# Five `h` tiles instead of four, the `y` sums in the spent half of `u`, a shorter gate, and 360 fill products instead of 480

## The chip, the cores and the metric

The kernel runs on one core of a Trainium2 chip. The metric is the device time of one execution in microseconds. Before the change it is 3912.99 us, the median of three runs (3912.96 to 3919.06). A core has five engines with instruction streams of their own, each worked off in order: PE (TensorE: matrix products; its weight loads are listed as PEld), DVE (VectorE), ACT (ScalarE), POOL (GpSimd) and SP (SyncE), which in this kernel issues every DMA. Engines wait for each other through semaphores.

## What is computed

The input `x` is eight sequences of 512 tokens with 256 channels, all in float32. Four residual layers follow each other:

```python
x = x + attn_a(layernorm(x))   # latent attention, 16 heads, rotary tables, causal softmax
x = x + ffn(layernorm(x))      # gate, up and down products (704 wide), inputs and weights rounded to FP4 blocks
x = x + attn_b(layernorm(x))   # a state-space layer, both directions in time
x = x + ffn(layernorm(x))      # the same weights again
```

The change lies in the state-space layer:

```python
xz = layernorm(x) @ in_w;  xs, z = split(xz)          # 512 channels each
for each direction d (forward, backward):
    xc = silu(causal_conv(xs))
    dt, B, C = split(xc @ xproj_w)                    # 64, 16 and 16 columns
    dt = softplus(dt @ dt_w + dt_b)
    h[t] = exp(dt[t] * A) * h[t-1] + dt[t] * B[t] * xc[t]     # 512 channels x 16 states
    y_d[t] = sum over the 16 states of h[t] * C[t]  +  xc[t] * D_skip
y = concat(y_fwd, y_back) @ merge_w * silu(z)         # silu(z) is the gate
x = x + residual + y @ out_w
```

## The kernel before

**Threads.** The program is written as Python generators that are interleaved: one for attention (`attention`, `heads`), one for feed-forward layers, the input half of the state-space layer and its merge (`ffns`, `mamba_pre`, `merge`), and one for the scans (`ssm`, with `ssm_prep` for what a scan needs). While sequence `b` is scanned, attention for `b + 3` and feed-forward layers of other sequences are spread between its steps. What they record is not yet the final order.

**The planner.** `issue_in_order` (L138) takes the whole recorded program and makes the order of each engine by hand, as a list scheduler. It derives dependences from the memory that instructions read and write, gives each a duration from a table (`cost`, L96) and a rank (the longest remaining path), and lets the instruction with the highest rank that is ready go next. It then ties each engine to that order. So any change of a duration class, of a ring's depth or of a dependence can reorder all engines.

**Rings.** Tiles come from rings, by tag: a tile waits until all users of the tile that many places before it are done. `h` has four tiles of 128x1024 float32, `u` three, `rep0` and `rep1` three each, `tmpB` three, `yt` one of 128x512. In PSUM, the eight banks are split as `pa` 2, `pb` 2, `a` 2, `y` 1, `ub` 1.

**A scan step.** For each sequence and direction there are four column blocks `m` of 128 channels, each with eight steps of two states: 512 steps in all. A step does the following:

- SP loads the rows of B and C for two states, replicated to 128 partitions (`rep0`, `rep1`; L1059, 512 KB each).
- DVE multiplies `ub` (a PSUM copy of `u = dt * xc`, made by ACT at L1077 at the start of each `m`) by `rep0` into an `h` tile (L1081).
- ACT makes two exponentials (L1084), and DVE runs two scans in place in the `h` tile (L1086 the forward direction, L1088 the backward one).
- POOL multiplies the tile by `rep1` (L1095).
- PE adds its eight 128x128 parts, transposed, into the bank `y` (L1098). The `h` tile is free then.

After eight steps ACT copies `y` into the tile `yt` (L1102), PE transposes it back in four products into a bank `a` (L344, called at L1105), DVE adds `xc * D_skip` (L1106), and SP stores the result.

**Preparation of a scan.** `ssm_prep` loads the convolved input of a direction as two `u` tiles of two column blocks each (L1015, two loads for each sequence and direction, 32 in all). The x-projection (L314 into `a`, with `tmpA` and `u`) reads both of them. Then dt follows (L1038 to L1051), and `u` is multiplied by dt in place (L1052). A `u` tile is used by two column blocks, `m % 2` of 0 and 1; its last reader is the copy into `ub` (L1077) of the second.

**The gate.** In `mamba_pre`, for the four column blocks of `z`, a product lands in a `pb` bank `o`. ACT makes `th = tanh(0.5 * (o + bias))` (L965) and `zb = o + bias` (L967), and DVE closes with `(th + 1) * zb` (L968) from two SBUF tiles. The convolution above it (`conv`, L928 to L930) already has another form: tanh, then plus one on ACT, and DVE reads PSUM.

**Fill products.** 480 products of constants (L1189, 128x512 bf16, nothing reads them) are recorded first. Their output is the first tile of the ring `y`:

```python
    FILL, FILL_FROM, FILL_GAP = 480, 70000, 600
...
    idle = psum("y")
    for _ in range(FILL):
        PE.matmul(idle.rearrange("p (a k) -> p a k", a=NT), idb, idb[:, None, :].to_broadcast([P, NT, P]), start=True, stop=True)
```

The planner gives them the lowest rank, and number `c` may not be planned ahead of 70 us + `c` * 0.6 us of its own clock.

Of the kernel before, what the change touches and what calls it, by code (L numbers as in the profile page):

```python
# [11 lines left out]
F32 = mybir.dt.float32  # L12
# [4 lines left out]
AF = mybir.ActivationFunctionType  # L17
ALU = mybir.AluOpType
AX = mybir.AxisListType

P = 128
T = 512
# [37 lines left out]


DMA_LAT = 2300


def accesses(i):
# [24 lines left out]
def ways(i):  # L90

    outer = [next((c for _, c in a.bass_ap.ap if c > 1), 1) for a in list(i.ins) + list(i.outs)]
    return max(k for k in range(1, 17) if all(x % k == 0 for x in outer))
# [44 lines left out]
def issue_in_order(tc, traced, rings, idle):  # L138
# [8 lines left out]
    hist, users, writers = {}, {}, {}  # L147
    for k, i in enumerate(ops):
        for name, lo, hi, p0, p1, _, psum, wr in acc[k]:
            h = hist.setdefault(name, [])  # L150
# [45 lines left out]
    port = [shared_port(i, a) for i, a in zip(ops, acc)]  # L196
    dma = [type(i).__name__ == "InstDMACopy" for i in ops]
    rank = [0.0] * n
    for k in reversed(range(n)):
        rank[k] = costs[k][1] * (1.2 if ops[k].engine == mybir.EngineType.DVE else 1.0) + DMA_LAT * dma[k] + max([rank[j] for j in succ[k] + behind[k]], default=0.0)  # L200
    at = [0.0] * n
    for c, k in enumerate(users[idle[0]]):
        rank[k], at[k] = -1.0, idle[1] + idle[2] * float(c)
# [9 lines left out]
    for _ in range(n):  # L213
        best = None
        for e, q in later.items():
            r, t = ready.setdefault(e, []), free.get(e, 0.0)
            while q and q[0][0] <= t:
                k = heapq.heappop(q)[1]
# [7 lines left out]
        while q and q[0][0] <= t:  # L226
            k = heapq.heappop(q)[1]
            heapq.heappush(r, (-rank[k], k))
        k = heapq.heappop(r)[1]
# [3 lines left out]
        if dma[k]:  # L233
            t = max(t, flying[0])
            m = ways(ops[k])
            lines[:m] = [max(t + 800, x) + costs[k][1] for x in lines[:m]]
            end = max(lines[:m]) + DMA_LAT - 800
            heapq.heapreplace(flying, end)
# [32 lines left out]
def tile_hybrid(ctx: ExitStack, tc: tile.TileContext, w: dict, consts: bass.AP, out: bass.AP):  # L271
    nc = tc.nc
    V, S, G, PE = nc.vector, nc.scalar, nc.gpsimd, nc.tensor
# [8 lines left out]
    cnt = [0]  # L282
    PB, TB, HB, QB, QA, HT = 2, 4, 3, 2, 2, 1
    LAG, TC, XB = 2, 3, 3
    NHB, NU, NDT, TA, RB, YT = 4, 3, 2, 2, 3, 1

    def const(shape, dt, tag):
        return cp.tile(shape, dt, tag=tag, name=tag)

    rings = {}  # L290

    def ringed(tag, bufs, t):
        rings.setdefault(tag, (bufs, []))[1].append(t.name)
        return t

    def work(shape, dt, tag, bufs=2):
        cnt[0] += 1
        return ringed(tag, bufs, wk.tile(shape, dt, tag=tag, name=f"{tag}_{cnt[0]}", bufs=bufs))
# [191 lines left out]
    def stats(src, th, twice=False):  # L490


        st = work([P, NT, 6], F32, "lnst" + th, 2)
        mv = work([P, NT, 2], F32, "lnmv" + th, 2)
        for i in range(NT):
            V.bn_stats(st[:, i, :], src[:, i, :])
        for i in range(NT):
            V.bn_aggr(mv[:, i, :], st[:, i, :])
        n = NT * (2 if twice else 1)
        ve = work([P, n], F32, "lnve" + th, 2)  # L500
        r = work([P, n], F32, "lnr" + th, 2)
        G.tensor_scalar(ve[:, :NT], mv[:, :, 1], EPS, None, ALU.add)
        if twice:
            G.tensor_scalar(ve[:, NT:], mv[:, :, 1], 1.0 + EPS, EPS * EPS, ALU.mult, ALU.add)
        newton_rsqrt(r, ve, n, th)
        return mv, r

    def shift(mv, r, th):
        nm = work([P, NT], F32, "lnnm" + th, 2)
        G.tensor_scalar(nm, mv[:, :, 0], -1.0, None, ALU.mult)  # L510
        G.tensor_tensor(nm, nm, r, ALU.mult)
        return nm

    def normalise(dst, src, r, nm):
        for i in range(NT):
            S.activation(dst[:, i, :], src[:, i, :], AF.Identity, bias=nm[:, i : i + 1], scale=r[:, i : i + 1])
# [5 lines left out]
    def token_transpose(dst, src, tag="pb"):  # L522

        for ct in range(2):
            o = psum(tag)
            for i in range(NT):
                transpose(o[:, i * P : (i + 1) * P], src[:, i, ct * P : (ct + 1) * P])
            S.copy(dst[:, ct, :], o)
# [332 lines left out]
    bin_ = const([P, 8], F32, "bin")  # L861
    binh = const([P, 8], F32, "binh")
# [69 lines left out]
    def mamba_pre(src, scr):  # L932
        xn = work([P, NT, C], F32, "fxn", 1)
        nc.sync.dma_start(xn, src.rearrange("(a p) c -> p a c", p=P))
        mv, r = stats(xn, "m", twice=True)
        nm, nm2 = shift(mv, r[:, :NT], "m"), shift(mv, r[:, NT:], "m2")
        r1 = work([P, NT], F32, "lnr1", 2)
        G.tensor_scalar(r1, r[:, :NT], 1.0, None, ALU.add)
        for i in range(NT):
            x3 = work([P, C], F32, "xrf", XB)  # L940
            S.activation(x3, xn[:, i, :], AF.Identity, bias=nm[:, i : i + 1], scale=r1[:, i : i + 1])
            nc.sync.dma_start(scr["x3"][i * P : (i + 1) * P, :], x3)
        normalise(xn, xn, r[:, NT:], nm2)
        yield
        xT = work([P, 2, T], F32, "fxT", 2)
        token_transpose(xT, xn)
        yield
        for m in range(8):
            wp = work([P, 2, P], F32, "xrf", XB)
            nc.sync.dma_start(wp, win_d[m])  # L950
            o = psum()
            for ct in range(2):
                mm(o, wp[:, ct, :], xT[:, ct, :], start=(ct == 0), stop=(ct == 1))
            if m < ND:
                xs = xsb[m % 2]
                S.activation(xs[:, 3 : 3 + T], o, AF.Identity, bias=bin_[:, m : m + 1])
                yield
                for d in range(2):
                    xb = work([P, T], F32, "tmpB", TC)
                    conv(d, m, xs, xb)  # L960
                    nc.sync.dma_start(scr["xc"][4 * d + m], xb)
                    yield
            else:
                th = work([P, T], F32, "tmpB", TC)
                S.activation(th, o, AF.Tanh, bias=binh[:, m : m + 1], scale=0.5)  # L965
                zb = work([P, T], F32, "tmpB", TC)
                S.activation(zb, o, AF.Identity, bias=bin_[:, m : m + 1])  # L967
                V.scalar_tensor_tensor(zb, th, 1.0, zb, ALU.add, ALU.mult)  # L968
                nc.sync.dma_start(scr["sz"][m - ND], zb)
                yield  # L970

# [94 lines left out]
    def ssm(b, d, scr):  # L1066


        for m in range(ND):
            if m % 2 == 0:  # L1070
                dt, u, _ = prep.pop((b, d, m // 2))
            while len(reps) < RB - 1:
                reps.append(load_rep(*todo_rep.pop(0), 0))
                repc.append(load_rep(*todo_c.pop(0), 1))
            y = psum("y")
            ub = psum("ub")
            S.copy(ub, u[:, m % 2, :])  # L1077
            for n in range(NS // 2):
                rb, rc = reps.pop(0), repc.pop(0)
                h = work([P, 2, T], F32, "h", NHB)  # L1080
                V.tensor_tensor(h, ub[:, None, :].to_broadcast([P, 2, T]), rb, ALU.mult)  # L1081
                for e in range(2):
                    a = psum("a")
                    S.activation(a, dt[:, m % 2, :], AF.Exp, scale=Aneg[:, d, m, 2 * n + e : 2 * n + e + 1])  # L1084
                    if d == 0:
                        V.tensor_tensor_scan(h[:, e], a, h[:, e], 0.0, ALU.mult, ALU.add)  # L1086
                    else:
                        V.tensor_tensor_scan(h[:, e, ::-1], a[:, ::-1], h[:, e, ::-1], 0.0, ALU.mult, ALU.add)  # L1088
                if todo_rep:
                    reps.append(load_rep(*todo_rep.pop(0), 0))  # L1090
                    repc.append(load_rep(*todo_c.pop(0), 1))
                if n == 2:
                    xp = work([P, T], F32, "xp", 1)
                    nc.sync.dma_start(xp, scr["xc"][4 * d + m])
                G.tensor_tensor(h, h, rc, ALU.mult)  # L1095
                for e in range(2):
                    for i in range(NT):
                        PE.matmul(y[:, i * P : (i + 1) * P], h[:, e, i * P : (i + 1) * P], ident,  # L1098
                                  start=(n == 0 and e == 0 and i == 0), stop=(n == NS // 2 - 1 and e == 1 and i == NT - 1), is_transpose=True)
                yield  # L1100
            yt = work([P, T], F32, "yt", YT)
            S.copy(yt, y)  # L1102
            o = psum("a")
            for q in range(NT):
                transpose(o[:, q * P : (q + 1) * P], yt[:, q * P : (q + 1) * P])  # L1105
            V.scalar_tensor_tensor(xp, xp, Dh[:, d, m : m + 1], o, ALU.mult, ALU.add)  # L1106
            nc.sync.dma_start(scr["y"][4 * d + m], xp)
# [70 lines left out]
                        pass  # L1178

    NA_, NB_, NS_ = 80, 100, 80  # L1180
    FILL, FILL_FROM, FILL_GAP = 480, 70000, 600
    PREP_AT, PREP_EV = 2, 2
    prep = {}
    af = {}
# [21 lines left out]
    first = thread_s(0)  # L1206
# [39 lines left out]
```

## Time and profile before

| what | value |
|---|---|
| median of the runs | 3912.99 us |
| profiled execution, its own time | 3908.11 us |
| its span, first to last instruction | 3906.3 us |
| mean granted PE clock | 0.903 |
| PE busy | 3215.2 us, 82% |
| DVE busy | 2953.2 us, 76% |
| POOL busy | 2111.9 us, 54% |
| ACT busy | 1740.7 us, 45% |
| DMA | 898.19 MB, mean 230 GB/s |

The profile is one execution, seen by the hardware profiler. A row of a group of instructions reads: line of the kernel, engine, operation, output <- input by the program's tile names, shapes, count | busy us, mean ns of one | idle time of the engine just ahead of them, and what ended most of it. A row of waits reads: who waited <- for whom: us in total, number of waits, the longest. Products on PE are pipelined and their ends are modelled, and a float32 product shows as two records, so PE's busy time is near to, but not the same as, the time it holds the engine. The granted clock is PE's, as a share of full speed.

### The profile page before, as it was taken

The numbers are of one execution on the slowest core, as the hardware profiler recorded it, in microseconds if no ns is written. First come the engines' busy times: TensorE is split into PE (matmuls) and PEld (weight loads), VectorE is DVE, ScalarE is ACT, GpSimd is POOL, SyncE is SP. The second block draws the span as 40 slices with busy tenths as digits, with TensorE's granted clock in tenths as the row PEclk, the third lists the DMA queues.
The fourth block names the chain that finished last, engine by engine and source line by source line (L and its number), as shares of the span: only waits on it lengthen the run. The fifth ranks groups of instructions, "written<-read, shape, count | busy, mean of one in ns | idle before, by whom it ended". The sixth has DMA issues, their size and how long they took to land. (4 is left out here: it accounts for less than half of the span.)

```text
span 3906.3 us, 43657 instructions
## 1 busy us (share of the span) xinstructions
PE 3215.2 (82%) x13444; PEld 1843.7 (47%) x13444; DVE 2953.2 (76%) x3803; ACT 1740.7 (45%) x2989; POOL 2111.9 (54%) x1714
## 2 busy tenths in 40 slices
PE   5999999798889888798778888798878767767676
PEld 3444444444444545455444554445444544444553
DVE  5325256878988689886987779887888988888873
ACT  2222343555465344453455444554455445543421
POOL 4103134665675466654775546655576676666642
PEclk7999999899989988899889998799888978978888
DMA  6222354888777977689667896779767886995942
GB/s 167 82 80 69 121 192 131 269 282 271 232 263 257 304 241 238 212 274 294 218 222 231 258 297 204 245 254 315 236 218 261 290 314 215 326 352 174 366 151 71
DMA packets 439799, 898.19 MB, mean 230 GB/s; under 512 B 65005, under 2 KB 220046, under 8 KB 439566
## 3 DMA queue, kind: packets, MB, share of 16 engines
q1 hardware_dynamic: 439566, 895.40, 69.3%
q8 instruction: 108, 1.77, 0.2%
q14 instruction: 125, 1.02, 0.1%
HBM read 783.61 MB, written 103.15 MB: 227 GB/s over the span
## 5 line engine op out<-in xcount | busy, mean ns | idle before, releaser
L1095 POOL TENSOR_TENSOR h<-h,rep 128x1024 f32<-128x1024 f32 x512 | 1217.1, 2383 | 856.5 <-DVE h L1088 303.9
L1084 ACT ACTIVATE a<-dt,Aneg 128x512 f32<-128x512 f32 x1024 | 697.7, 689 | 561.4 <-DVE h L1088 265.1
L1098 PE MATMUL y<-cst,h 128*128 128x128 f32 x4096 | 693.5, 298 | 180.2 <-POOL h L1095 179.6
L1081 DVE TENSOR_TENSOR h<-ub,rep 128x1024 f32<-128x1024 f32 x512 | 616.6, 1210 | 206.7 <-PE y L1098 95.2
L1098 PEld LDWEIGHTS y<-cst,h 128*128 128x128 f32 x4096 | 529.7, 153 | 412.9 <-POOL h L1095 236.3
L1086 DVE TENSOR_TENSOR_SCAN h<-a,h 128x512 f32<-128x512 f32 x512 | 601.3, 1206 | 52.4 <-ACT a L1084 46.6
L1088 DVE TENSOR_TENSOR_SCAN h<-a,h 128x512 f32<-128x512 f32 x512 | 600.1, 1208 | 48.1 <-ACT a L1084 40.9
L314 PE MATMUL pb<-wgu,fxT 128*128 128x512 f32 (+1 forms) x768 | 372.9, 596 | 23.0 <-DVE hff L804 14.1
L699 PE MATMUL pa<-pt,vs 128*32 128x128 f32 (+3 forms) x1024 | 371.1, 458 | 13.0 <-ACT pt L694 10.3
L314 PE MATMUL pb<-qv,hff 128*128 128x256 f32 x1024 | 303.0, 422 | 85.3 <-DMA qv<-sy 74.6
L694 ACT ACTIVATE pt<-pa 128x512 f32<-128x512 f32 x320 | 190.3, 595 | 350.0 <-PE pa L691 347.8
L927 PE MATMUL pb<-xs,tmpB 128*128 128x512 f32 x512 | 272.6, 652 | 41.1 <-DMA tmpB<-dg_d 31.1
L658 PE MATMUL pa<-kst,qst 96*128 96x512 f32 (+3 forms) x512 | 211.2, 456 | 60.3 <-DVE mx L668 32.7
L314 PEld LDWEIGHTS pb<-qv,hff 128*128 128x128 f32 x1024 | 194.9, 209 | 137.9 <-issue 57.0
L314 PE MATMUL pb<-wdn,hT 128*128 128x256 f32 (+1 forms) x768 | 228.4, 420 | 18.1 <-ACT hT L821 7.1
L689 PE MATMUL pa<-qst,kst 98*128 98x512 f32 (+3 forms) x512 | 227.5, 449 | 14.3 <-ACT pt L694 12.2
L668 DVE TENSOR_REDUCE mx<-pa 128x1 f32<-128x512 f32 (+2 forms) x384 | 179.9, 501 | 61.4 <-PE pa L660 60.9
L314 PEld LDWEIGHTS pb<-wgu,fxT 128*128 128x128 f32 x768 | 134.3, 199 | 126.2 <-issue 85.5
L689 PEld LDWEIGHTS pa<-qst,kst 98*128 98x128 f32 x512 | 100.7, 197 | 180.8 <-issue 106.3
L314 PEld LDWEIGHTS pb<-wdn,hT 128*128 128x128 f32 (+1 forms) x768 | 142.5, 206 | 72.2 <-issue 28.4
L658 PEld LDWEIGHTS pa<-kst,qst 96*128 96x128 f32 x512 | 105.8, 209 | 133.7 <-DVE mx L668 43.1
L927 PEld LDWEIGHTS pb<-xs,tmpB 128*128 128x128 f32 x512 | 95.5, 208 | 132.7 <-issue 83.9
(217 smaller groups left out, 4882.3 us busy)
## 6 DMA issues: line engine op xcount, KB each, us to landing
rep<-bcd SPq DMA_DIRECT2D x1024, 512.0 KB
hld<-hl SPq DMA_DIRECT2D x64, 512.0 KB
hff<-in_merge_w SPq DMA_DIRECT2D x128, 256.0 KB
qv<-sy SPq DMA_DIRECT2D x128, 256.0 KB
kst<-hld SPq DMA_DIRECT2D x192, 128.0 KB
qst<-hld SPq DMA_DIRECT2D x192, 128.0 KB
tmpB<-dg_d SPq DMA_DIRECT2D x64, 256.0 KB
sxc<-tmpB SPq DMA_DIRECT2D x64, 256.0 KB
```

The source lines that it names most:

```text
L314: PE.matmul(o, L, R, start=start, stop=stop, **kw)
L658: PE.matmul(o[:, at : at + n], qst[pr][:96, j, i * P : (i + 1) * P], kst[:96, j, :n], start=(k == 0), stop=False)
L689: PE.matmul(o[:, at : at + n], kst[:, j, kt * P : (kt + 1) * P], qst[pr][:, j, kt * P :], start=(k == 0), stop=False)
L694: S.activation(pt, o, AF.Exp)
L699: PE.matmul(po[c : c + 32, kt * P :], vs[:, kt, h * VW : h * VW + 32], pt[:, at : at + n], start=(kt == 0), stop=(kt == 2), tile_position= ...
L927: PE.matmul(o, dg[:, k, :], xs[:, at : at + T], start=(k == 0), stop=(k == 3))
L1081: V.tensor_tensor(h, ub[:, None, :].to_broadcast([P, 2, T]), rb, ALU.mult)
L1084: S.activation(a, dt[:, m % 2, :], AF.Exp, scale=Aneg[:, d, m, 2 * n + e : 2 * n + e + 1])
L1086: V.tensor_tensor_scan(h[:, e], a, h[:, e], 0.0, ALU.mult, ALU.add)
L1088: V.tensor_tensor_scan(h[:, e, ::-1], a[:, ::-1], h[:, e, ::-1], 0.0, ALU.mult, ALU.add)
L1095: G.tensor_tensor(h, h, rc, ALU.mult)
L1098: PE.matmul(y[:, i * P : (i + 1) * P], h[:, e, i * P : (i + 1) * P], ident, start=(n == 0 and e == 0 and i == 0), stop=(n == NS // 2 - 1 a ...
```

## The change

- The ring of `h` has five tiles instead of four.
- The tile `yt` and its ring are gone. ACT copies `y` into the half of the tile `u` that belongs to the column block just scanned; the transposes read it there. So a `u` tile is in use until the transposes of its second column block.
- The gate makes `zb = tanh(...)`, then `zb + 1` on ACT, and DVE closes with `(o + bias) * zb`, with `o` in PSUM. One `tmpB` tile for each gate is no longer used.
- There are 360 fill products instead of 480.
- A constant `FIRST` is added to the rank of the first multiply into `h`. It is 0.

```diff
+FIRST = 0.0
...
+    first = min(users[name][0] for name in rings["h"][1])
     for k in reversed(range(n)):
         rank[k] = costs[k][1] * (1.2 if ops[k].engine == mybir.EngineType.DVE else 1.0) + DMA_LAT * dma[k] + max([rank[j] for j in succ[k] + behind[k]], default=0.0)
+        if k == first:
+            rank[k] += FIRST
...
-    NHB, NU, NDT, TA, RB, YT = 4, 3, 2, 2, 3, 1
+    NHB, NU, NDT, TA, RB = 5, 3, 2, 2, 3
...
-                th = work([P, T], F32, "tmpB", TC)
-                S.activation(th, o, AF.Tanh, bias=binh[:, m : m + 1], scale=0.5)
                 zb = work([P, T], F32, "tmpB", TC)
-                S.activation(zb, o, AF.Identity, bias=bin_[:, m : m + 1])
-                V.scalar_tensor_tensor(zb, th, 1.0, zb, ALU.add, ALU.mult)
+                S.activation(zb, o, AF.Tanh, bias=binh[:, m : m + 1], scale=0.5)
+                S.activation(zb, zb, AF.Identity, bias=1.0)
+                V.scalar_tensor_tensor(zb, o, bin_[:, m : m + 1], zb, ALU.add, ALU.mult)
...
-            yt = work([P, T], F32, "yt", YT)
+            yt = u[:, m % 2, :]
             S.copy(yt, y)
...
-    FILL, FILL_FROM, FILL_GAP = 480, 70000, 600
+    FILL, FILL_FROM, FILL_GAP = 360, 70000, 600
```

## The prediction

> **What bounds the kernel now.** I first read the busy shares by stretch of time (start:end, length, busy us and number of instructions for PE, PEld, DVE, ACT and POOL, then granted PE clock, DMA share, GB/s), cut where the trace changes character: 642 us is the first `y` product (L1098), 792 us the 33rd `h` multiply (L1081), 3780 us the last `y` product.
>
> ```profile
> 300.00:642.00 342.00, 332.76 (x1260) 146.94 (x1259) 156.10 (x305) 123.62 (x232) 92.18 (x126) 1.00 0.38 119
> 642.00:792.00 150.00, 121.37 (x571) 70.09 (x571) 120.68 (x153) 82.77 (x140) 94.43 (x76) 0.91 0.81 254
> 792.00:3780.00 2988.00, 2424.33 (x10249) 1451.22 (x10247) 2525.34 (x3030) 1446.17 (x2407) 1827.54 (x1340) 0.89 0.77 259
> ```
>
> There are two regimes. Up to 642 us PE is busy 97% at full clock and DVE under half: PE sets the time. From 792 us to 3780 us DVE is busy 84.5% and PE 81%: neither is full, and the two hold each other up through the `h` tiles. The last 126 us hold no scan; the order of work there is the same in both programs, so I leave them out.
>
> Second view: the fill products of L1189 alone, in the head.
>
> ```profile
> 90.00:300.00 210.00, 90.29 (x345) 30.20 (x345) 0.99 0.26 84
> 300.00:642.00 342.00, 36.62 (x136) 12.14 (x135) 1.00 0.38 119
> ```
>
> They are planned for moments in which PE has nothing else, but the last one runs at 641.5 us and the first `y` product at 642.0. The first POOL product (L1095, 558.4 us, 2.4 us long) had been ready since 561 us. The cause is in the code: the fill tile is the first tile of the ring `y`, which has one bank, so no `y` product may precede the last fill.
>
> Third view: what ended the waits of DVE between 640 and 3780 us (total us, times, longest).
>
> ```profile
> DVE h L1081 <- PE y L1098: 95.2, 33, 12.5
> DVE h L1081 <- DMA rep<-bcd: 64.9, 31, 5.8
> DVE h L1086 <- ACT a L1084: 46.6, 44, 3.0
> DVE h L1088 <- ACT a L1084: 40.9, 39, 3.1
> ```
>
> The first row is the shortage of `h` tiles: the multiply waits until PE has consumed the tile of four steps before. It is the largest row of DVE and still only 95 of about 490 us in which DVE idles in that stretch. The second row stands right behind it. Last, four groups by line (busy us, mean ns of one, idle before):
>
> ```profile
> L1095 POOL TENSOR_TENSOR h<-h,rep 128x1024 f32<-128x1024 f32 x512 | 1217.1, 2383 | 856.5 <-DVE h L1088 303.9
> L1098 PE MATMUL y<-cst,h 128*128 128x128 f32 x4096 | 693.5, 298 | 180.2 <-POOL h L1095 179.6
> L1081 DVE TENSOR_TENSOR h<-ub,rep 128x1024 f32<-128x1024 f32 x512 | 616.6, 1210 | 206.7 <-PE y L1098 95.2
> L1189 PE MATMUL y<-idb 128*128 128x512 bf16 x480 | 126.9, 381 | 0.0
> ```
>
> **The change part by part.** The sum is made against the profiled execution, 3908.1 us (span 3906.3). The median is 3913.0, so 4.9 are added at the end.
>
> *120 fills fewer.* Eight fills back to back take 1.89 us from 571.57 us on, the last of them 0.38 to its end, so one holds PE for (1.89 - 0.38) / 7 = 0.216 us; by busy time it is 36.62 / 136 = 0.269. So 120 x 0.216 = 26 us, or 32. The orders of the two built programs are equal on PE up to the 360th fill (place 920 among the matrix products); the missing 120 all lay behind it, in the stretch where PE waits for next to nothing (97% busy). Lower bound 0 (each product would then wait for its operand instead), upper bound 26 + 29: in 642 to 792 us PE idles 150 - 121.4 = 28.6 us, which smoother work could also win. I take 26, full, because that row says PE.
>
> The first `y` product moves from place 1855 to 1528: past the 120 fills and 207 others. The first dt product (L1038) now runs at 531.5 us, and 29 us later the first POOL product is done; 83 of the 120 fills lay ahead of L1038, 18 us, so the first `y` product would stand near 531.5 - 18 + 29 = 543 us instead of 642. But this is not 100 us gained. In DVE's order the 33rd L1081 has the same number of rows ahead of it in both programs (699), and on PE the 257th `y` product has the same other work ahead of it except the fills, within 3 us. The attention work that stepped back is done among the first 32 scan steps. From there on only the fills are gone.
>
> [...]
>
> *Fifth `h` tile.* The wait of L1081 then goes to the `y` products of five steps before. One step takes (3780 - 642) / 512 = 6.1 us, the mean wait is 95.2 / 33 = 2.9 us, so most of it could go; outside the first 150 us (11.4 of the 95) it is 84 us. What is late next: the replicated rows (`rep<-bcd`, ring of three, 64.9 us) and the two exponentials (46.6 and 40.9). POOL's products do not get faster. In DVE's order the new program even runs the multiply ahead of its scans less often (345 of 512 multiplies with no other unscanned tile, against 303), so the extra tile lies mostly behind POOL. Bounds 0 and 84. As DVE and PE are nearly equally busy and the next row is close, I take a third: 28.
>
> *Gate.* L968 reads two SBUF tiles, 32 times, median 828 ns, mean 1198, longest 2843: it shows large delays. In its place comes the form of L930 (PSUM and SBUF in, 64 times, 721 to 751 ns, mean 743). So 32 x (1.198 - 0.743) = 14.6 us of DVE; ACT's second pass becomes L929's form, 630 instead of 681 ns, 1.6 us less. The PSUM bank is held until DVE has read it: PE waited 19.6 us for L930 in 64 convolutions, which is 9.8 for 32 gates, against 12.6 for L967 now; nothing there. Of 14.6 us off an engine that is busy 84.5%, half, 7 us (bounds 0 and 15). [...]
>
> *`yt` into `u`.* The copy (L1102) and the four transposes are the same, on the same engines, at 0.585 us and 49.0 / 64 = 0.77 us. What moves is when `u` comes free. Before, its last reader was the copy to `ub` (L1077) at the start of its second column block; now it is the transposes eight steps later, some 49 us. In the built program 25 of 32 loads of `u` (L1015) wait for PE where none did, standing in SP's queue with `rep` loads behind them. The x-projection (L314 into `a`, x16), which needs the last of them, keeps its place among the `y` products, often exactly behind the step that frees the tile (step 80.0, 112.0, 144.0). From the last POOL product to the free tile it takes 693.5 / 512 = 1.4 us of `y` products, 0.6 of copy, 0.8 of transposes, then 512 KB at 259 GB/s, 2.0 us. So PE may now stand at the x-projection, and all its queue behind it. The nearest row is PE's wait for the `qv<-sy` loads, 66.3 us in 35 waits, mean 1.9, longest 8.4. Some 14 x-projections (the first periods had free tiles): 14 x 1.9 = 27 us of PE. Lower bound 0, upper 14 x 8.4 = 118. As PE is busy 81%, half counts: 13 us lost.
>
> `FIRST` is 0 and adds nothing. Sum: -26 - 28 - 7 + 13 = -48; 3908.1 - 48 = 3860, and 3865 as a median.
>
> **The rivals.** *The fifth tile gives all:* 84 us of waits go and `u` costs nothing: 26 + 84 + 15 = 125, median 3788. For it: the row is the largest of DVE. Against it: the other rows stand close behind, and PE must take up the pace.
>
> *The fills were hidden anyway and the new order spends the rest:* the removed products only make others wait, and the planner, which reorders every engine, lets the tile's gain go. For it: the order is made from a table of durations that differ from the trace. Then 0 to 40 us are gained; I put it at 20, median 3893, a part of it within 0.2% of no change.
>
> *Slower: the `u` load stops PE and SP.* If the x-projection comes a whole step (6.1 us) late each time, PE loses 14 x 6.1 = 85 us, `rep` loads queue behind the `u` load on SP, and the tile's gain is eaten by it: 85 - 26 - 7 = +52, median 3965. It decides from (26 + 28 + 7) / 14 = 4.4 us of lost time for each x-projection. For it: no slack left in the orders named above. Against it: the dt chain behind has some 15 steps before its result is used, and PE idles 19%.
>
> **How the numbers follow.** The forecast 0.50 (own range 3830 to 3890); the fifth tile gives all 0.12; little gained 0.20, of which 0.13 still over 0.2% faster; slower through `u` 0.18. What can be told from no change is about 0.2%, 8 us. Faster 0.50 + 0.12 + 0.13 = 0.75, same 0.07, slower 0.18. The range 3805 to 3935 leaves out half of the first rival and over half of the last, some 0.16.
>
> **What would show it.** In the new profile: the first `y` product near 543 us, PE over 95% busy before it and still at clock 1.00; the 33rd L1081 near 792 - 26 = 766 us; DVE's wait for PE `y` at a third or less of 95 us, while the waits for `rep` and `a` grow; the gate's last line at 0.74 us each; PE's wait at L314 for the `u` load at 20 to 40 us. Wrong if the 33rd L1081 stays at 790, if the clock in the head falls, if PE waits for `u` over 60 us, or if the wait for `y` stays with five tiles.

## The result, and the profile after

The changed kernel takes 3968.6 us (median of 4 runs, 3959.5 to 3973.6), against 3913.0 us before: a ratio of 1.0139, 95% interval 1.0121 to 1.0156. It is 1.4% slower where 1.2% faster was forecast. Lines of the changed kernel are three or four higher than before: L1084 is the `h` multiply (L1081 before), L1089 and L1091 are the scans, L1098 POOL's product, L1101 the `y` products, L1105 ACT's copy of `y` into `u` (L1102 into `yt` before), and L1080 the copy of `u` into `ub` (L1077).

Engines and groups on the page of the changed kernel:

```profile
span 3968.5 us, 43304 instructions
PE 3206.5 (81%) x13324; PEld 1843.0 (46%) x13324; DVE 2931.9 (74%) x3803; ACT 1738.7 (44%) x2989; POOL 2110.6 (53%) x1714
...
L1098 POOL TENSOR_TENSOR h<-h,rep 128x1024 f32<-128x1024 f32 x512 | 1212.6, 2373 | 893.5 <-DVE h L1091 315.0
L1101 PE MATMUL y<-cst,h 128*128 128x128 f32 x4096 | 689.6, 298 | 208.5 <-POOL h L1098 207.8
L1084 DVE TENSOR_TENSOR h<-ub,rep 128x1024 f32<-128x1024 f32 x512 | 615.0, 1206 | 177.2 <-DMA rep<-bcd 61.9
```

No engine has more work than before: PE has 9 us less, DVE 21 us less, POOL 1 us less. All of the 62 us in which the span grew are idle time. The idle time ahead of the `h` multiply even fell, from 206.7 to 177.2 us, while that of POOL's product and of the `y` products rose by 37 and 28 us. Waits of DVE between 640 and 3843 us:

```profile
DVE h L1084 <- DMA rep<-bcd: 61.9, 33, 8.1
DVE h L1091 <- ACT a L1087: 50.0, 45, 3.4
DVE h L1084 <- PE y L1101: 42.6, 14, 11.0
DVE tmpB L993 <- PE pb L318: 40.9, 10, 20.2
DVE mx L672 <- PE pa L664: 40.7, 26, 9.0
...
DVE h L1084 <- ACT ub L1080: 23.8, 15, 4.0
```

The row that the fifth tile was to shorten did fall: the wait for the `y` products went from 95.2 to 42.6 us. (Whether the tile did that is taken up further below.) The time is lost elsewhere, and no row of this view names it.

**Where the time went.** The starts of all `h` multiplies in both traces, 512 steps, are cut here at the 64 column blocks (eight steps each). "Gap" is the time from the last multiply of a block to the first of the next; "odd" is the second block of a `u` tile (`m` = 1 or 3). Means in us:

| | first block | gap into odd | in odd block | gap into even | in even block | two blocks in all | first to last multiply |
|---|---|---|---|---|---|---|---|
| before | 112.2 | 6.9 | 42.6 | 5.5 | 43.6 | 98.6 | 3218 |
| after | 32.1 | 17.8 | 35.7 | 5.4 | 44.2 | 103.1 | 3281 |

The column before the last is the sum of the four means left of it. The 33rd multiply, the first of the fifth block, starts 10.0 us earlier than before (786.6 against 796.6 us). From there to the last multiply it takes 3049.4 us instead of 2975.4, 74.0 more, and the rest behind it 1.8 less: these three make the 62 us.

Two things changed. The first block is 80 us shorter: its `y` products, which stand behind the last fill in both kernels, begin at 562.4 us instead of 642.0. And the gap into each odd block is 10.9 us longer, 32 times, of which the block itself makes good 6.9. The gap into even blocks did not move. So the place is the border between the two blocks that share a `u` tile.

This is such a border in the changed kernel, the one after the multiply at 3696.72 us (start, us, engine, line, operation; idle before in brackets), on ACT:

```profile
3705.53 1.14 ACT L1051 ACTIVATE tmpA<-tmpA,neg 128x1024 f32<-128x1024 f32 x1
3711.97 0.59 ACT L1105 COPY u<-y 128x512 f32<-128x512 f32 x1 [5.31 <-PE y L1101]
3712.46 0.60 ACT L1080 COPY ub<-u 128x512 f32<-128x512 f32 x1
```

and on DVE:

```profile
3706.82 0.40 DVE L1007 TENSOR_TENSOR xrf<-pb,xrf 128x256 f32<-128x256 f32 x1
3713.14 2.36 DVE L1084 TENSOR_TENSOR h<-ub,rep 128x1024 f32<-128x1024 f32 x2 [5.93 <-POOL tmpA L1053]
```

The multiply of the next block needs `ub`. The copy into `ub` stands behind the copy of `y` on ACT, and that one waits until scans, POOL's product and the eight `y` products of the last step are done. The same border before the change, where the last multiply started at 3641.89 us, on ACT:

```profile
3645.24 0.57 ACT L1077 COPY ub<-u 128x512 f32<-128x512 f32 x1
3645.75 1.05 ACT L1047 ACTIVATE tmpA<-tmpA 128x1024 f32<-128x1024 f32 x1
3646.84 1.15 ACT L1048 ACTIVATE tmpA<-tmpA,neg 128x1024 f32<-128x1024 f32 x1
3651.08 0.58 ACT L1102 COPY yt<-y 128x512 f32<-128x512 f32 x1 [3.09 <-PE y L1098]
```

and on DVE:

```profile
3646.98 1.20 DVE L1081 TENSOR_TENSOR h<-ub,rep 128x1024 f32<-128x1024 f32 x1
```

There `ub` is copied first, 5.8 us ahead of `y`, and the next block's multiplies run (from 3646.98 us) while the old block drains. Note that the trace puts the 5.93 us of DVE's wait down to POOL, since a wait for several semaphores goes to the one that came last by the profile, and that at other borders other work of DVE fills the gap. That is why only 23.8 us stand in the row of `h` waiting for ACT's `ub`.

The order is not forced by data, as the two halves of `u` differ. It comes from the planner, which holds the users of one ring tile on one engine in program order:

```python
    for name, ks in users.items():
        prev = {}
        ks = ks if name in owner else writers.get(name, ())
        for k in dict.fromkeys(ks):
            if ops[k].engine in prev:
                after[prev[ops[k].engine]].append(k)
            prev[ops[k].engine] = k
```

Before, ACT's users of a `u` tile were its two copies into `ub`. Now the copy of the first block's `y` is recorded between them. In the built orders the second copy into `ub` stands ahead of the first block's `y` copy at 32 of 32 such borders before, and at none after. At the borders into an even block, which reads another `u` tile, the copy into `ub` stands ahead at 31 of 31 in both.

### The profile page after: what moved, and what is told of

It reads as the page before. It is cut to its first block, busy times and chain, and to the rows that moved or that the text cites. A ratio compares the mean times of both kernels' runs of the same rounds, so it can differ in the third digit from the quotient of the medians.

```text
span 3968.5 us, 43304 instructions
## 1 busy us (share of the span) xinstructions
PE 3206.5 (81%) x13324; PEld 1843.0 (46%) x13324; DVE 2931.9 (74%) x3803; ACT 1738.7 (44%) x2989; POOL 2110.6 (53%) x1714
## 5 line engine op out<-in xcount | busy, mean ns | idle before, releaser
L1098 POOL TENSOR_TENSOR h<-h,rep 128x1024 f32<-128x1024 f32 x512 | 1212.6, 2373 | 893.5 <-DVE h L1091 315.0
L1087 ACT ACTIVATE a<-dt,Aneg 128x512 f32<-128x512 f32 x1024 | 699.3, 689 | 622.4 <-DVE h L1089 296.3
L1101 PE MATMUL y<-cst,h 128*128 128x128 f32 x4096 | 689.6, 298 | 208.5 <-POOL h L1098 207.8
L1084 DVE TENSOR_TENSOR h<-ub,rep 128x1024 f32<-128x1024 f32 x512 | 615.0, 1206 | 177.2 <-DMA rep<-bcd 61.9
L1101 PEld LDWEIGHTS y<-cst,h 128*128 128x128 f32 x4096 | 529.1, 153 | 424.7 <-POOL h L1098 259.2
L1091 DVE TENSOR_TENSOR_SCAN h<-a,h 128x512 f32<-128x512 f32 x512 | 601.3, 1206 | 57.1 <-ACT a L1087 50.0
L1089 DVE TENSOR_TENSOR_SCAN h<-a,h 128x512 f32<-128x512 f32 x512 | 602.5, 1206 | 42.5 <-ACT a L1087 35.5
L703 PE MATMUL pa<-pt,vs 128*32 128x512 f32 (+3 forms) x1024 | 372.6, 460 | 11.6 <-ACT pt L698 9.2
L931 PE MATMUL pb<-xs,tmpB 128*128 128x512 f32 x512 | 284.3, 678 | 44.1 <-DMA tmpB<-dg_d 25.1
```

The source lines that it names most:

```text
L703: PE.matmul(po[c : c + 32, kt * P :], vs[:, kt, h * VW : h * VW + 32], pt[:, at : at + n], start=(kt == 0), stop=(kt == 2), tile_position= ...
L931: PE.matmul(o, dg[:, k, :], xs[:, at : at + T], start=(k == 0), stop=(k == 3))
```

## The experiments

Theory B says that this order on ACT at 32 borders makes the loss. Its rivals: F (the missing fills), U (the late load of `u`, the slower case of the prediction), H (five `h` tiles lead to a worse plan as such), R (any new plan costs or gains tens of us by chance). Ratios are to the kernel before, run on the same chip, as its own median moved between 3913 and 3929 us from one set of runs to the next.

**e1: the changed kernel with 480 fills.**

```diff
-    FILL, FILL_FROM, FILL_GAP = 360, 70000, 600
+    FILL, FILL_FROM, FILL_GAP = 480, 70000, 600
```

> The changed kernel with 480 fill products again: five h tiles, y's sums in u and the gate stay. Theory F (the loss comes with the missing fills: PE's clock falls in the head, and the early start of the scans spoils the stretch behind it): back to 3905 to 3920 us or below. Theory U (the loss comes from the late release of u): stays at 3960 to 3980 us. Theory R (every new plan costs some tens of us by chance): anything from 3890 to 3970.

Measured: 3985.4 us, ratio 1.0154 (1.0128 to 1.0180). F falls: with the fills back the loss stays.

**e2: 360 fills alone, in the kernel before.**

```diff
-    FILL, FILL_FROM, FILL_GAP = 480, 70000, 600
+    FILL, FILL_FROM, FILL_GAP = 360, 70000, 600
```

> The kernel before with 360 fill products, nothing else. Theory F: about 3965 us, most of the 55 us of loss, with the clock down between 400 and 600 us as in the changed kernel. Theory U: 3885 to 3913 us, as the 26 us forecast or nothing. Theory R: anything in between.

Measured: 3914.2 us, ratio 0.9979 (0.9963 to 0.9995). Fewer fills gain 8 us, not 26, and do not harm. By the starts of its multiplies, the first block shrinks from 112.2 to 36.9 us. But at the 33rd multiply only 3 us of that lead are left (793.7 against 796.6 us), and from there to the last multiply both take the same time (2975.6 and 2975.4 us). So the early start is paid back within the first four blocks, as the prediction said of it.

**e3: the last 120 fills made short, the order kept.** The planner's cost of a fill is pinned to its old value, so that every engine keeps its order (only the width of 120 products differs).

```diff
+    fills = set(users[idle[0]])
+    costs = [(25 + 0.41 * 512, 85 + 0.41 * 512) if k in fills else c for k, c in enumerate(costs)]
...
-    for _ in range(FILL):
-        PE.matmul(idle.rearrange("p (a k) -> p a k", a=NT), idb, idb[:, None, :].to_broadcast([P, NT, P]), start=True, stop=True)
+    for c in range(FILL):
+        if c < 360:
+            PE.matmul(idle.rearrange("p (a k) -> p a k", a=NT), idb, idb[:, None, :].to_broadcast([P, NT, P]), start=True, stop=True)
+        else:
+            PE.matmul(idle[:, :16], idb, idb[:, :16], start=True, stop=True)
```

> The kernel before with all 480 fills and the order of every engine kept; but the last 120 fills are 16 columns wide instead of 512, so that they hold PE for next to nothing. It takes PE's time off without a new order. My forecast's step (PE sets the time of the head, so 26 us go): 3887 us. Theory F in its clock form (the fills stand in idle time and keep the clock up): 3913 to 3930 us and a clock below 1.0 between 400 and 600 us. Theory R: 3905 to 3913 us, no loss without a new order.

Measured: 3934.3 us, ratio 1.0033 (1.0013 to 1.0054). Taking PE's time off without a new order does not gain 26 us; it loses about 13. The stretches (length, busy us of PE, PEld, DVE, ACT and POOL, then clock, DMA share, GB/s), in the kernel before:

```profile
400.00:500.00 100.00, 97.97 (x371) 43.17 (x370) 23.31 (x55) 35.96 (x68) 11.05 (x39) 1.00 0.40 124
500.00:600.00 100.00, 97.11 (x347) 40.18 (x346) 53.95 (x94) 49.34 (x83) 39.35 (x42) 0.98 0.58 183
```

and with the short fills:

```profile
400.00:500.00 100.00, 90.16 (x365) 42.05 (x365) 22.03 (x53) 33.87 (x65) 11.05 (x39) 0.97 0.40 118
500.00:600.00 100.00, 90.78 (x324) 38.11 (x323) 50.95 (x89) 48.99 (x81) 37.99 (x41) 0.91 0.56 183
```

PE is less busy, its granted clock falls (from 1.00 and 0.98 to 0.97 and 0.91), and in the same 200 us it gets through 29 records fewer. The fills hold PE 18.4 us less in these two stretches (7.1 instead of 25.5), and its busy time falls by 14.1: most of the time that they left became idle. The rest, and more, was lost where the granted clock was low. In the trace with short fills it is 0.50 in four stretches between 431 and 588 us, 23.9 us in all, against one of 3.4 us before. The longest of them, first in the kernel before, then with the short fills:

```profile
574.40:587.90 13.50, 13.50 (x49) 4.89 (x47) 5.16 (x10) 5.71 (x11) 2.73 (x1) 1.00 0.71 207
574.40:587.90 13.50, 11.13 (x38) 4.00 (x36) 6.37 (x11) 4.14 (x8) 3.03 (x2) 0.50 0.65 229
```

From one and the same record of PE to another, these four stretches take 26.6 us, and 19.1 in the kernel before. That is all of the 7.3 us by which the last fill is later (648.8 against 641.5 us).

**e4: five `h` tiles and `y` in `u`, the old gate, 480 fills.**

```diff
-    NHB, NU, NDT, TA, RB, YT = 4, 3, 2, 2, 3, 1
+    NHB, NU, NDT, TA, RB, YT = 5, 3, 2, 2, 3, 1
...
-            yt = work([P, T], F32, "yt", YT)
+            yt = u[:, m % 2, :]
```

> The kernel before with five h tiles and y's sums in u (five tiles do not fit beside the tile yt), 480 fills, the old gate. Theory F: 3880 to 3913 us. Theory U: 3960 to 3975 us, with waits of PE for the u load. Theory R: anything from 3890 to 3970. My forecast's step for the two together was 28 - 13 = 15 us faster, 3898 us.

Measured: 4000.7 us, ratio 1.0197 (1.0178 to 1.0216). The loss lies in these two parts; with the other two, in the changed kernel, it is smaller (1.0139).

**e5: `y` in `u` alone.**

```diff
-            yt = work([P, T], F32, "yt", YT)
+            yt = u[:, m % 2, :]
```

> The kernel before with y's sums put into u, nothing else (four h tiles, 480 fills, the old gate). Theory B (the planner keeps the users of a ring's tile on one engine in program order; so ACT copies the second column block of u into ub only after it has copied the first block's y sums into u, and the scans run dry at 32 of 64 block boundaries): 3950 to 4000 us. Theory U (the late load of u): also slower, with PE waiting at the x-projection. Theory H (five h tiles as such lead to a worse plan): 3905 to 3920 us.

Measured: 4000.6 us, ratio 1.0197 (1.0166 to 1.0228). H falls: the loss is there in full with four tiles. The gap into odd blocks is 16.2 us, into even ones 5.6. In its trace no wait of PE at the x-projection was ended by the load of `u` (in that of the changed kernel neither, but two, 9.6 us together, name no releaser); what it waited for there was DVE:

```profile
PE a L314 <- DVE h L1086: 12.9, 4, 8.7
```

12.9 us against 10.8 before. This speaks against U, and e6 decides.

**e6: the changed kernel, with the second copy into `ub` recorded first.**

```diff
-            ub = psum("ub")
-            S.copy(ub, u[:, m % 2, :])
+            if m % 2 == 0:
+                ub = psum("ub")
+                S.copy(ub, u[:, 0, :])
+            else:
+                ub = ub2
...
+            if m % 2 == 0:
+                ub2 = psum("ub")
+                S.copy(ub2, u[:, 1, :])
             yt = u[:, m % 2, :]
```

> The changed kernel, but the copy of the second column block of u into ub is recorded ahead of the first block's copy of y into u, so that ACT may do it first as in the kernel before. u is still held until its last transposes. Theory B: 3860 to 3915 us, all or most of the loss gone. Theory U and theory H: no change, 3955 to 3980 us.

Measured: 3910.4 us, ratio 0.9967 (0.9944 to 0.9989). All of the loss goes, with `u` held as long as in the changed kernel and its loads as late: counted in `h` multiplies, each of the 32 loads starts within four of its place in the changed kernel, and on average seven later than in the kernel before. The gap into odd blocks is 6.5 us. B holds, U falls.

**e7: the changed kernel, with `y` in the last `h` tile instead of `u`.**

```diff
-            yt = u[:, m % 2, :]
+            yt = h[:, 0, :]
```

> The changed kernel, but y's sums go into the h tile of the block's last step instead of u. So u comes free as early as before, nothing stands between the two copies into ub, and one of five h tiles is held some 3 us longer once in eight steps. Theories B and U: 3860 to 3915 us. Theory H: 3955 to 3980 us. If e6 stays slow and this is fast, it is U.

Measured: 3923.0 us, ratio 0.9990 (0.9969 to 1.0012). Another way round the same order, and the loss is gone too; but there is no gain.

**e8: the gate alone, in the kernel before.**

```diff
-                th = work([P, T], F32, "tmpB", TC)
-                S.activation(th, o, AF.Tanh, bias=binh[:, m : m + 1], scale=0.5)
                 zb = work([P, T], F32, "tmpB", TC)
-                S.activation(zb, o, AF.Identity, bias=bin_[:, m : m + 1])
-                V.scalar_tensor_tensor(zb, th, 1.0, zb, ALU.add, ALU.mult)
+                S.activation(zb, o, AF.Tanh, bias=binh[:, m : m + 1], scale=0.5)
+                S.activation(zb, zb, AF.Identity, bias=1.0)
+                V.scalar_tensor_tensor(zb, o, bin_[:, m : m + 1], zb, ALU.add, ALU.mult)
```

> The kernel before with the new gate alone. My forecast's step: 7 us faster, bounds 0 and 15, so 3898 to 3913 us. Theory R (a new plan costs or gains tens of us by chance): outside of that.

Measured: 3923.5 us, ratio 0.9989 (0.9971 to 1.0007): 4 us, the interval holds no change.

**e9: the gate and 360 fills, with four `h` tiles and the tile `yt`.** The diffs of e2 and e8 together.

> The kernel before with the new gate and 360 fills: four h tiles and the tile yt. Against e6 and e7 it lacks only the fifth tile. If the fifth tile is worth the 28 us of my forecast, this is some 28 us slower than e7; if the tile is worth nothing, it is at e6 and e7 within 10 us, 0.99 to 1.00 of the kernel before.

Measured: 3917.0 us, ratio 0.9982 (0.9964 to 1.0000). It stands between e6 (0.9967) and e7 (0.9990), which differ from it by the fifth tile and by where `y` goes. So the fifth tile gains nothing that these intervals can show. Between e9 and e7, where `u` comes free as early as before, they leave it an estimated 8 us at most, against the forecast's 28.

**e10: `y` in `u` alone, with the second copy into `ub` recorded first.** The diffs of e5 and e6 together, on the kernel before.

> As e5 (y's sums in u, nothing else changed), but the copy of the second block into ub is recorded ahead of the first block's copy of y into u. Theory B: back to the kernel before within 0.4%, from e5's 2.0% slower. Theory U (the late u load): 1% or more slower still. Here the fifth tile, the gate and the fills can't cover for it.

Measured: 3933.9 us, ratio 1.0023 (1.0000 to 1.0046). From 2.0% slower to 0.2%, by the place of one copy alone. What may be left for the late load of `u` and the rest is 0 to 0.5%.

**e11: only the planner's table.**

```diff
-DMA_LAT = 2300
+DMA_LAT = 2310
```

> The kernel before with one number of the planner's table changed (2310 instead of 2300 ns of DMA latency), which computes and moves the same and only reorders. It shows how much a new order is worth by chance. Theory R wants 10 us or more of difference, either way; otherwise within 8 us of the kernel before.

Measured: 3936.5 us, ratio 1.0020 (1.0003 to 1.0037). This new order alone costs 0.2%, and the differences of e2, e8, e9 and e10 from 1 are of the same size. One order does not bound R. But the traces of all versions part cleanly: where the second copy into `ub` stands ahead at all 32 borders (e2, e3 and e6 to e12), the ratio is within 0.33% of 1; where it stands ahead at none (the changed kernel, e1, e4 and e5), it is 1.0139 to 1.0197.

**e12: e6 with four `h` tiles and a fourth `rep0` tile.** The planner's loads for `rep0` run one step further ahead.

```diff
-    NHB, NU, NDT, TA, RB = 5, 3, 2, 2, 3
+    NHB, NU, NDT, TA, RB = 4, 3, 2, 2, 3
+    RB0 = 4
...
-        rep = work([P, 2, T], F32, f"rep{k}", RB)
+        rep = work([P, 2, T], F32, f"rep{k}", RB if k else RB0)
...
-            while len(reps) < RB - 1:
+            while len(reps) < RB0 - 1:
                 reps.append(load_rep(*todo_rep.pop(0), 0))
+            while len(repc) < RB - 1:
                 repc.append(load_rep(*todo_c.pop(0), 1))
```

> As e6 (the changed kernel with the early copy into ub), but with four h tiles, and the room of the fifth given to a fourth tile of the ring rep0. It asks whether the row behind the h tiles, the wait of the h multiply for rep, is the better place for the room. If that row (62 to 79 us of DVE's waits) were on the path, 15 to 40 us faster than e6; if waits only move on to the next row, within 10 us of e6.

Measured: 3919.9 us, ratio 0.9987 (0.9967 to 1.0008). Within 10 us of e6: the next row is no better place for the room. The row itself nearly went (L1089 is the `h` multiply here; in e6 the wait for `rep` is 78.5 us):

```profile
DVE h L1089 <- PE y L1107: 89.9, 45, 6.8
DVE h L1089 <- issue: 41.8, 20, 8.6
DVE h L1089 <- DMA rep<-bcd: 6.9, 4, 3.2
```

Of all versions only e2 and e6 have an interval that lies wholly below the kernel before. e6, the changed kernel with one copy moved, is the fastest by its median ratio (0.9967), but not told apart from e2 (0.9979) or e9.

## Why the prediction was wrong

**`yt` into `u`: this is the step that failed.** It said: "What moves is when `u` comes free." It followed the reads of `u` (the transposes, and the loads that wait for them) and left out that the tile gained a writer on ACT. The copy of `y` into `u` became a user of the tile between its two copies into `ub`, and a rule of the planner, the one shown above, tied the second one behind it. The price was put at 13 us, with an upper bound from PE's wait for loads. It was 2.0% of the kernel before (e5), some 77 us, by another way: the scans waited for `ub`. The prediction went by the places of the `y` products, the x-projection and the loads in the two orders; the order of the two copies on ACT would have told it: 32 of 32 against none.

**The slower rival** was put at 3965 us, and 3968.6 was measured; this is chance. Its mechanism, the load of `u` that stops PE and SP, does not happen to that extent: 9.6 us of PE at most in the changed kernel's trace, and e6 is fast with those loads.

**The fifth tile** was put at 28 us and is worth nothing that can be seen: e4 and e5 have the same ratio, and e6 and e7 stand around e9. The row did shrink in the changed kernel, 95.2 to 42.6 us, but this does not show the tile at work. In e11, with four tiles and nothing but a new order, the row is as short, and the kernel is no faster:

```profile
DVE h L1081 <- DMA rep<-bcd: 71.5, 35, 5.4
DVE h L1081 <- PE y L1098: 50.6, 29, 9.6
```

In e6, with five tiles and without the late `ub`, it is 70.2 us, and the wait for `rep` rose from 64.9 to 78.5 (L1087 is the `h` multiply there):

```profile
DVE h L1087 <- DMA rep<-bcd: 78.5, 44, 4.5
DVE h L1087 <- PE y L1104: 70.2, 28, 8.7
DVE h L1094 <- ACT a L1090: 49.3, 48, 3.5
```

"The next row is close" was right, but it is not the whole reason: e12, with four `h` tiles again, takes that next row down to 6.9 us, the first stands at 89.9, and nothing is gained either. A row of waits is no sum to be won. What would set the pace of the scans with both rows gone, no run here shows.

**The fills** were put at "26, full, because that row says PE". The row said 97% busy, and part of that busy time was the fills themselves: without their 36.6 us it is 87%. e3 shows that PE's time was not the limit there: the same order with 120 short fills is 0.33% slower. In e2, without them, the gain is 8 us. Here the granted clock changed too, for which the sum had nothing; that it falls in the head was one of the prediction's own signs of being wrong. In the changed kernel the same stretches read:

```profile
400.00:500.00 100.00, 93.91 (x304) 40.97 (x303) 20.54 (x52) 34.37 (x64) 11.13 (x39) 0.86 0.38 118
500.00:600.00 100.00, 85.62 (x288) 37.52 (x287) 58.28 (x91) 53.14 (x84) 43.66 (x42) 0.88 0.66 209
```

The granted clock fell from 1.00 and 0.98 to 0.86 and 0.88. In the six rows for these two stretches (the kernel before, e3, the changed kernel) it is 1.00 and 0.98 with PE busy 97.97 and 97.11 us, and 0.86 to 0.97 in the four with less. The busy share does not order it: the lowest clock stands beside 93.91 us, and in e2 it is 1.00 between 400 and 500 us with 92.24. What sets it, no run here shows. Of the 13.6 us by which the profiled execution of e3 is longer than that of the kernel before, the stretches at 0.50 make 7.5; where the rest comes from is open.

**The start of the scans.** The first `y` product came at 562.4 us (543 forecast, 642 before), and the 33rd multiply at 786.6 us (796.6 before; I had read 792 from a coarser view and forecast 766). That the early start would be paid back was right: the second block starts 60 us earlier than before (612.7 against 672.5 us), the fifth 10 us. But it is not the missing 120 fills alone that bring it. With all 480 and another order the first `y` product comes at 574.2 us in e1 and 576.9 in e8.

**The gate.** L971 takes 737 ns against 743 forecast and 1198 before, 14.7 us less of DVE. Its share of the time, 7 us by the forecast, is 4 us with an interval that holds nothing (e8). Next to the slow borders it looks like more: e1 has it and stands at 1.0154, e4 has not and stands at 1.0197.

## What to carry to other kernels

Where a scheduler keeps the users of a tile in program order, putting a result into a spent tile is not free storage: list who uses that tile on each engine before and after, and look in the built order whether a late instruction now stands ahead of an early one. Read idle time by place as well as by releaser: the starts of one repeated instruction, cut at the borders of the loop, showed a gap that was 10.9 us longer, on average, at every second border, which no row of waits named. A long row of waits is not a gain in store: here two such rows became shorter, one in e11 and one in e12, and the time did not follow. And an engine that is busy with fill work is not thereby the bound: subtract the fills first.

## What was not expected of the hardware

Products that nothing reads were worth keeping at full width: made 16 columns wide instead of 512, with every engine's order kept, the last 120 of them left a kernel 0.33% slower (interval 0.13 to 0.54%), with PE's granted clock at 0.91 instead of 0.98 between 500 and 600 us and four stretches at 0.50, over which the same products took 7.5 us longer. That holds for this order: with the 120 left out and the order made anew (e2), the kernel was 0.21% faster (0.05 to 0.37%).
